# Four small reorderings in a four-layer graph kernel: tile 0's y2T, the hyperedge aggregate, layer 2's bias and the last output tile

## The chip, the cores and the metric

The kernel runs on one core of one Trainium2 chip. The metric is the device time of one execution in microseconds; the kernel before took 1214.8 us, the median of three runs from 1214.73 to 1215.12. A core has a matrix engine (TensorE, PE in the profile, with its weight loads listed as PEld), a vector engine (VectorE, DVE), a scalar engine (ScalarE, ACT), a general engine (GpSimd, POOL) and a queue that issues transfers (SyncE, SP). Each engine works through its own instructions in order and waits for the others on semaphores.

## The reference, cut to what matters

The input x has 8 batches of 2048 nodes with 64 features, and adj is a row-normalised 2048 x 2048 adjacency. Four graph layers follow each other, each with a residual and a layer norm over the 64 features:

```python
x = layernorm(x + chebyshev(x, adj))            # layer 0: out = sum_k T_k(adj) x W_k(node), k = 0, 1, 2
x = layernorm(x + hypergraph_attention(x, H, adj))   # layer 1
x = layernorm(x + x @ Ws + (adj @ x) @ Wn + bias)    # layer 2
x = layernorm(x + (A_hat @ x) @ W3.T)           # layer 3, A_hat = D^-1/2 (adj + I) D^-1/2
```

In layer 0, T_2 x = 2 adj (adj x) - x, and the weights of each node come from an embedding of 16 numbers. In layer 1, each of 64 hyperedges first gets an aggregate: the softmax-weighted mean of its nodes' features h, here a sum over nodes (`aggp`) times the reciprocal of the weights' sum (`rden`). Scores of the edges are computed from ELU(aggregate) through a linear layer and a tanh, and weight what every node takes from its edges. A second term, `industry`, is adj @ (x W_ind).

## The kernel before, in words

Nodes are cut into 16 tiles of 128 rows; a tile holds 8 x 64 = 512 columns (batch and feature). The adjacency is used as a mask of zeros and ones (`msk`, kept in DRAM for the later layers) times a row scale, and every left operand is split into a high and a low part (`y_hi`, `y_lo`), so that one product of a tile with the adjacency is 32 matmuls of 128 x 512: 16 row blocks times two parts.

Layer 0 begins with the first product y1 = adj x for all tiles (line 569), and the second product of tile 0 (line 603). Then `layer0` goes tile by tile inside `program_order()`, which fixes the order on PE, DVE, ACT and POOL as it is written. For tile 0, POOL forms mask times row scale in four quarters (`scaled_first`, line 1340) and DVE compares each with the raw adjacency (`compare_first`, line 1350), which only feeds a flag that is read at the end of the program. `second_term` (lines 1415 to 1421) transposes tile 0's y2 on PE into `try` and subtracts xT on DVE, which gives `y2T`. `weigh` (lines 1448 and 1459) then does eight groups for each tile: PE multiplies xT, y1T and y2T by the weights into a two-buffer PSUM tile `pp`, and DVE adds four slices of it to r, weighted by the embedding. The raw adjacency halves of tile 2 take the buffers of tile 0's, so they are loaded by SP once tile 0's comparisons are done. SP is not in the fixed order; the scheduler places its transfers.

Layer 0's last tile goes through `last_tile`, which ends with `rden` and the last parts of h, y_hi and y_lo (line 1599, two instructions for each half). Layer 1 starts with the list `head`, whose chain on one tile is: `agg` (line 731), exp (735), ELU (738), transpose (trhe), copy, linear layer (fche, 755), tanh, scores; pieces `0.i` and `1.i` of the industry product are put between. Its main list runs the 16 tiles as a software pipeline and ends with layer 2's projection, so that x2 holds the residual plus the self term, and with 16 POOL instructions that add layer 2's bias to x2 (line 1254).

Layer 2 and layer 3 are plain loops over the tiles, placed by the scheduler. Each step of layer 2 loads a mask tile, does 32 matmuls into `acc`, computes r on DVE (line 2029), normalises it (`layernorm`, lines 139 to 156: sum, centring, square on ACT, variance, root on ACT, reciprocal, product), and projects the tile before (`projected`: transposes tr_l, the copy xT_l at line 1994, matmuls yp at line 2008). Each step of layer 3 does 32 matmuls, r (line 2042), the same layer norm into `o`, and a store of `o` that ACT issues (line 2047).

Of the kernel before, what the change touches and what calls it, by code (L numbers as in the profile page):

```python
# [9 lines left out]
F32 = mybir.dt.float32  # L10
# [3 lines left out]
ALU = mybir.AluOpType  # L14
# [44 lines left out]
def r_(ap):  # L59
    return ap.bitcast(F32R)  # L60
# [3 lines left out]
def kernel(  # L64
# [58 lines left out]
    def b_view(t2):  # L123
        return t2.rearrange("p (b c) -> p b c", b=B)

    def bcast(small):
        return small.unsqueeze(2).to_broadcast([P, B, C])
# [484 lines left out]
    def layer1(  # L612
# [86 lines left out]
        def column_view(src):  # L699
            return src[:, 2 * P:4 * P].rearrange("p (b e) -> p b e", b=B)[:, :, 0]  # L700

        head = (
            "1.mask 2.mask 3.mask 4.mask c.agg 0.i c.hexp c.he 0.ind c.trhe c.agg1 c.heT "
            "c.fche c.sums c.the c.nagg 1.i c.sep 1.i c.serow c.sert 1.i c.ese c.eexp c.ese2 "
            "c.dnp c.ext 1.i c.rec c.hgr c.dnp2 1.i c.late "
        )
        with tc.tile_pool(name="fa", bufs=2) as fa:
# [8 lines left out]
                for n, k in (("ftr", 1), ("fmm", 1))  # L716
            )
            with program_order():
                c = {}
                low = slice(64, P)  # L720
                sums = fa.tile([P, 2, B], F32, tag="sums", name="sums", bufs=1)
                late = own.tile([P, NT - NE, 2, B], F32, tag="b0_11", name="rest_sums")
# [1 line left out]
                def parts(dst, full):  # L724

                    nc.vector.tensor_copy(r_(dst), full)
                    nc.vector.tensor_tensor(r_(dst[low]), full[low], dst[low], ALU.subtract)

                def aggregate():
                    c["agg"] = agg = fa.tile([P, BC], F32, tag="hs", name="agg", bufs=3)  # L730
                    nc.vector.tensor_tensor(b_view(agg), b_view(aggp), bcast(rden), ALU.mult)

                def exp_edges():
                    c["he"] = fa.tile([P, BC], F32, tag="xT", name="he")
# [93 lines left out]
                def other_weights():  # L828
# [1 line left out]
                    weight_sums(c["dn2"], NE, NT)  # L830

                perform(head, dict(
                    agg=aggregate, hexp=exp_edges, he=elu_edges, trhe=turn_edges, heT=turned_edges,
                    fche=fc_edges, the=tanh_edges, sep=edge_scores, serow=score_rows, sert=turn_rows,
                    agg1=lambda: parts(agg1, c["agg"]), sums=sum_edges, nagg=negated, ese=capped,
                    eexp=exp_scores, ese2=split_scores, dnp=first_weights, ext=extension,
# [274 lines left out]

        first = {}

        def layer2(j):

            t = {}

            def by_half(v):
                return v[:, j, :].rearrange("p (r h c) -> p h r c", h=2, c=C)

            def turned():
                t["tr"] = tr = ps_m.tile([P, BC], F32, tag="m", name=f"tr2_{j}")
                for pr in range(NP):
                    pc = slice(pr * P, (pr + 1) * P)
                    transpose(tr[:, pc], x2[:, j, pc])

            def kept_turned():
                t["xT"] = small("sT", f"xT2_{j}", (P, BC))
                nc.scalar.copy(t["xT"], t["tr"])

            def projected(place):
                pool, tag = dict(g=(ps_g, "g"), f=(ps_fc, "fc"))[place]
                mm = pool.tile([P, 2, BC], F32, tag=tag, name=f"u_{j}")
                t["mm"] = mm = mm.rearrange("p h (r c) -> p h r c", r=NP)
                for pr in range(NP):
                    for h in range(2):
                        rs = slice(h * 64, (h + 1) * 64)
                        nc.tensor.matmul(
                            mm[:, h, pr, :], t["xT"][rs, pr * P:(pr + 1) * P], w2_sb[rs],
                            start=True, stop=True,  # L1140
                        )

            def high():
                nc.scalar.copy(r_(by_half(i_hi)), t["mm"][:, :, :, 0:C])

            def with_self():
                nc.vector.tensor_tensor(
                    by_half(x2), t["mm"][:, :, :, C:2 * C], by_half(x2), ALU.add
                )

            def rest():
                nc.vector.tensor_tensor(
                    r_(by_half(i_lo)), t["mm"][:, :, :, 0:C], by_half(i_hi), ALU.subtract
                )

            def mask():
                first["a"] = mask_parts(own, 0, (0, 1, 2, 15), "l2")

            def times():
                if not j:  # L1160
                    first["acc"] = ps_acc.tile([P, BC], F32, tag="acc", name="a2_0")
                times_mask(first["acc"], first["a"], i_hi, i_lo, j)

            return dict(
                f=turned, xT=kept_turned, mm=projected, hi=high, add=with_self, lo=rest,
                amask=mask, A=times,
            )
# [4 lines left out]
        with program_order():  # L1172
# [77 lines left out]
                ),  # L1250
                {"rests": lambda: reciprocals(late[:, :, 0, :], late[:, :, 1, :], NE, NT)},
            )
            for j in range(NT):
                nc.gpsimd.tensor_tensor(
                    b_view(x2[:, j, :]), b_view(x2[:, j, :]),
                    bias2_sb.unsqueeze(1).to_broadcast([P, B, C]), ALU.add,
                )
        return x2, first["acc"]

    def mask_parts(own, j, homes, name):  # L1260

# [8 lines left out]
    def layer0(  # L1270
# [459 lines left out]
        def last_tile():  # L1730

            last = NT - 1
            early[0](6)
            half_features(0)
            gather(last - 1)
            denp = ps_p.tile([P, 2, 2, 4 * C], F32, tag="pp", name="denp")[:, 0, 0, 0:B]
            nc.tensor.matmul(denp, mds[last - 1], es[:, last - 1, :], start=True, stop=False)
            projected(last, 0)
            half_normed(1, 0)
            half_normed(1, 1)  # L1740
            copied(last, 0, "sc")
            weights_of(last, slice(0, 4))
            copied(last, 0, "h")
            copied(last, 0, "hi")
            half_normed(1, 2)
            half_weighted(0)
            copied(last, 0, "lo")
            early[0](3)
            half_features(1)
            early[0](1)  # L1750
            projected(last, 1)
            copied(last, 1, "sc")
            weights_of(last, slice(4, 8))
            half_weighted(1)
            early[0](1)
            half_gather(0)
            nc.tensor.matmul(denp, mds[last], es[:, last, :], start=False, stop=True)
            half_gather(1)
            nc.vector.tensor_tensor(rden, rden, denp, ALU.add)
            nc.vector.tensor_scalar(rden, rden, TINY, None, op0=ALU.max)  # L1760
            nc.vector.reciprocal(rden, rden)
            for what in ("h", "hi", "lo"):
                copied(last, 1, what)

        with program_order():
# [3 lines left out]
            quarters = [scaled_first(h) for h in range(2)]  # L1769
            compare_first(0, quarters[0])  # L1770
            mask(1, 1)
            compare_first(1, quarters[1])
            for h in range(2):
                summed(0, h)
            second_term(0)
            scaled(1, 0)
            for j in range(NT):
                when(j + 2, load_adj)
# [58 lines left out]
    def short_program(top):  # L1837
# [83 lines left out]
        with tc.tile_pool(name="l0", bufs=1) as l0, tc.tile_pool(  # L1921
# [49 lines left out]
                nc.vector.tensor_scalar(flag, bad[:, 0:1], -1.0, 1.0, op0=ALU.mult, op1=ALU.add)  # L1971


        x2, a2_first = layer1(
            own, wts, fcw_sb, fcb_sb, av_sb, fcg_sb, vecs, rden, hgr, aggp, agg_st, h_sb, y_hi,
            y_lo, mask_tile, times_mask, w2_sb, bias2_sb, ps_acc, early,
        )
# [2 lines left out]
        with tc.tile_pool(name="mj2", bufs=3) as mjp, tc.tile_pool(  # L1980
# [40 lines left out]
            for j in range(NT):  # L2021
                acc = a2_first
                if j:
# [5 lines left out]
                nc.vector.scalar_tensor_tensor(  # L2029
                    r, acc, cols_of["s1"][:, j:j + 1], x2[:, j, :], op0=ALU.mult, op1=ALU.add  # L2030
                )
                layernorm(ln, r, x2[:, j, :], f"l2_{j}")
                if j:
                    projected(j - 1)
            projected(NT - 1)
            for j in range(NT):
                a = mask_tile(mjp, j, "l3")
                acc = ps_acc.tile([P, BC], F32, tag="acc", name=f"a3_{j}")
                for mt in range(NT):
                    times_mask(acc, a, v_hi, v_lo, mt)  # L2040
# [615 lines left out]
```

## Time and profile before

| what | value |
|---|---|
| runs | 1214.73, 1214.8, 1215.12 us; median 1214.8 |
| the profiled execution | 1214.06 us, of which the span that the trace covers is 1212.4 us |
| mean granted PE clock | 0.994 of full speed |
| busy share: PE, PEld, DVE, ACT, POOL | 98%, 78%, 73%, 32%, 41% |
| HBM traffic over the span | 128 GB/s |
| landing of an adjacency half's DMA, median and longest | 3.8 and 12.5 us |
| landing of an output store, median | 2.0 us |

The page gives the share of the span in which an engine was busy. A matmul's end is modelled, so a busy PE can still be one that waits inside; the starts of its instructions tell its pace better. A line of a timeline shows when an instruction or a run of equal ones started, how long it took, its engine, its source line, what it wrote and read, and in brackets how long its engine stood idle before it and what ended that. The busy share of an engine is an average over stages with different limits; what an edit is worth is read at its own place.

### The profile page before, as it was taken

The page shows a single profiled execution, that of the slowest core. Times are in us where ns is not written, and L with a number is a line of the kernel's source. Part 1 is how long each engine was busy: PE and PEld are TensorE (multiplying, and loading weights), DVE is VectorE, ACT ScalarE, POOL GpSimd, SP SyncE. Part 2 cuts the span into 40 slices and gives each one's busy share as a digit, 9 for nine tenths or more (in the row PEclk, how much of TensorE's full clock was granted, in tenths as well). Part 3 has the DMA queues.
Part 4 walks back from the last instruction along what each step waited for, and adds up shares of the span by engine and source line. Part 5 has one row for each costly group of instructions (what it writes and reads, how often), then busy time and mean ns, then how long its engine had stood idle before and what let it go on. Part 6 is the DMA issues. An engine that isn't in the chain of part 4 may idle for free. (4 is left out here: it accounts for less than half of the span.)

```text
span 1212.4 us, 19761 instructions
## 1 busy us (share of the span) xinstructions
PE 1185.2 (98%) x7470; PEld 945.0 (78%) x7470; DVE 889.8 (73%) x1671; ACT 386.7 (32%) x1003; POOL 500.5 (41%) x429
## 2 busy tenths in 40 slices
PE   9999899999999999999999999999999999999996
PEld 7877688888888888888887766666657788888885
DVE  5555668888888888888877688988877665655554
ACT  3100101222222222222233467767777311111111
POOL 2000382555545555555521389888870700000000
PEclk9999999999999999999999899999999999999999
DMA  8987942323332233333293223223220433334451
GB/s 298 239 228 228 169 151 93 113 98 116 115 109 95 96 103 115 116 116 114 79 324 127 89 71 113 91 83 105 96 70 1 152 127 108 136 105 174 174 178 68
DMA packets 101848, 157.10 MB, mean 130 GB/s; under 512 B 13041, under 2 KB 64369, under 8 KB 96113
## 3 DMA queue, kind: packets, MB, share of 16 engines
q1 hardware_dynamic: 96944, 151.38, 38.8%
q10 hardware_dynamic: 4368, 4.33, 1.0%
q8 instruction: 61, 1.00, 0.3%
q0 software_dynamic: 432, 0.05, 0.1%
q14 instruction: 43, 0.34, 0.1%
HBM read 117.97 MB, written 37.76 MB: 128 GB/s over the span
## 5 line engine op out<-in xcount | busy, mean ns | idle before, releaser
L1459 DVE SCALAR_TENSOR_TENSOR r<-pp,emb_sb,r 128x256 f32<-128x256 f32 x512 | 247.5, 483 | 77.8 <-PE pp L1448 63.7
L1448 PE MATMUL pp<-w_sb,y2T 64*128 64x256 f32 x1024 | 153.4, 376 | 3.5 <-DVE y2T L1421 3.5
L1448 PE MATMUL pp<-w_sb,xT 64*128 64x256 f32 x1024 | 155.4, 380 | 0.6 <-DVE r L1459 0.6
L1448 PE MATMUL pp<-w_sb,y1T 64*128 64x256 f32 x1024 | 153.4, 376 | 0.0
L1317 POOL TENSOR_TENSOR ms<-msk,srow 128x1024 f32<-128x1024 f32 x30 | 76.6, 2553 | 93.7 <-DVE msk L449 93.7
L1448 PEld LDWEIGHTS pp<-w_sb,y2T 64*128 64x128 f32 x1024 | 99.2, 187 | 15.0 <-DVE y2T L1421 3.9
L1448 PEld LDWEIGHTS pp<-w_sb,y1T 64*128 64x128 f32 x1024 | 99.4, 187 | 11.2
L1448 PEld LDWEIGHTS pp<-w_sb,xT 64*128 64x128 f32 x1024 | 95.2, 187 | 12.9 <-issue 2.8
L569 PE MATMUL y1p<-x_hi,m 128*128 128x512 f32 x256 | 102.9, 402 | 0.0
L569 PE MATMUL y1p<-x_lo,m 128*128 128x512 f32 x256 | 100.6, 393 | 0.3 <-DVE x_lo L472 0.2
L1909 PE MATMUL a<-v_hi,mj_l 128*128 128x512 f32 x256 | 100.1, 392 | 0.0
L1909 PE MATMUL a<-v_lo,mj_l 128*128 128x512 f32 x256 | 100.0, 391 | 0.0
L1909 PE MATMUL a<-y_lo,mj_l 128*128 128x512 f32 x240 | 95.1, 396 | 0.0
L1909 PE MATMUL a<-y_hi,mj_l 128*128 128x512 f32 x240 | 94.9, 395 | 0.0
L1405 PE MATMUL y2p<-y_hi,msk 128*128 128x512 f32 x240 | 94.7, 395 | 0.0
L1405 PE MATMUL y2p<-y_lo,msk 128*128 128x512 f32 x240 | 93.5, 390 | 0.0
L1909 PE MATMUL ind<-y_hi,mj_l 128*128 128x512 f32 x208 | 90.5, 435 | 0.0
L1909 PE MATMUL ind<-y_lo,mj_l 128*128 128x512 f32 x208 | 81.9, 394 | 0.0
L1357 DVE SCALAR_TENSOR_TENSOR ms<-ms,adj 128x1024 f32<-128x1024 f32 x30 | 67.3, 2243 | 0.0
L968 POOL TENSOR_TENSOR ez<-ez,coef 128x1024 f32<-128x1024 f32 x32 | 61.6, 1927 | 11.1 <-DVE ez L963 11.0
L1640 POOL TENSOR_TENSOR hs<-h,es 128x512 f32<-128x512 f32 x15 | 15.7, 1043 | 116.1 <-ACT hgr L1612 116.1
L1909 PEld LDWEIGHTS ind<-y_hi,mj_l 128*128 128x128 f32 x208 | 39.3, 189 | 26.7 <-issue 17.3
(334 smaller groups left out, 2429.4 us busy)
## 6 DMA issues: line engine op xcount, KB each, us to landing
mj_l<-mask SPq DMA_DIRECT2D x44, 1024.0 KB, 4.9
adj<-in_at SPq DMA_DIRECT2D x64, 256.0 KB, 3.8
mask<-msk SPq DMA_DIRECT2D x32, 512.0 KB, 4.5
raw<-in_at SPq DMA_DIRECT2D x31, 512.0 KB, 5.6
oh<-oh SPq DMA_DIRECT2D x32, 128.0 KB, 4.1
xT<-in_xt SPq DMA_DIRECT2D x16, 256.0 KB, 3.1
xs<-in_xn SPq DMA_DIRECT2D x16, 256.0 KB, 2.7
kept<-x SPq DMA_DIRECT2D x16, 256.0 KB, 3.5
```

The source lines that it names most:

```text
L569: nc.tensor.matmul(accs[q][jj], r_(m[:, t, jj * P:(jj + 1) * P]), r_(part[:, mt, :]), start=i + h + t == 0 and part is x_hi, stop=i == 3 a ...
L968: nc.gpsimd.tensor_tensor(by_b(ezs[i]), by_b(ezs[i]), per_b(t["coef"], 2 * i, 2), ALU.mult)
L1317: nc.gpsimd.tensor_tensor(ms, m, srow[j].unsqueeze(1).to_broadcast([P, 8, P]), ALU.mult)
L1357: nc.vector.scalar_tensor_tensor(ms, ms, 1.0, raws[j][h], op0=ALU.mult, op1=ALU.not_equal, accum_out=bad[:, 2 * j + h:2 * j + h + 1],)
L1405: nc.tensor.matmul(acc, r_(msk[j, mt // 8][:, mt % 8, :]), r_(part[:, mt, :]), start=mt == 0 and part is y_hi, stop=mt == NT - 1 and part ...
L1448: nc.tensor.matmul(pp[:, h, pl, :], terms[j][name][rs, 2 * bq + pl], w_sb[rs, k, dq * 4 * C:(dq + 1) * 4 * C], start=k == 0, stop=k == K - 1,)
L1459: nc.vector.scalar_tensor_tensor(rb, ppv[:, :, dd, :], emb_sb[:, j, d:d + 1], rb, op0=ALU.mult, op1=ALU.add)
L1640: nc.gpsimd.tensor_tensor(b_view(hs), b_view(h_sb[:, j, :]), bcast(es[:, j, :]), ALU.mult)
L1909: nc.tensor.matmul(acc, r_(a[:, mt, :]), r_(part[:, mt, :]), start=mt == 0 and part is hi, stop=mt == NT - 1 and part is lo,)
```

## The change

It has four parts.

1. In layer 0, `second_term(0)` is called before the second pair of comparisons (`compare_first(1, ...)`) and after the second mask, in place of after both comparisons and the two sums on POOL.
2. The aggregate is computed in `last_tile`, directly after the reciprocal of `rden` and before the last parts of h, y_hi and y_lo. It lies in the buffer `b0_1` of the pool `own`, and `head` no longer has `c.agg`.
3. The bias of layer 2 is added on POOL to x2 for tiles 0 and 15 only, behind layer 1; for tiles 1 to 14 it is added on POOL to r, inside the loop of layer 2, between r and the layer norm.
4. The last tile of layer 3 is done in two halves of 256 columns (four batches each). Each half has its own 32 matmuls, its own layer norm on half-width tiles, and its own store; SP issues the first half's, ACT the second half's.

```diff
         head = (
-            "1.mask 2.mask 3.mask 4.mask c.agg 0.i c.hexp c.he 0.ind c.trhe c.agg1 c.heT "
+            "1.mask 2.mask 3.mask 4.mask 0.i c.hexp c.he 0.ind c.trhe c.agg1 c.heT "
...
-                c = {}
+                c = {"agg": early[2]}
...
+        def add_bias2(t):
+            nc.gpsimd.tensor_tensor(
+                b_view(t), b_view(t), bias2_sb.unsqueeze(1).to_broadcast([P, B, C]), ALU.add
+            )
...
-            for j in range(NT):
-                nc.gpsimd.tensor_tensor(
-                    b_view(x2[:, j, :]), b_view(x2[:, j, :]),
-                    bias2_sb.unsqueeze(1).to_broadcast([P, B, C]), ALU.add,
-                )
+            for j in (0, NT - 1):
+                add_bias2(x2[:, j, :])
...
             nc.vector.reciprocal(rden, rden)
+            agg = own.tile([P, BC], F32, tag="b0_1", name="agg")
+            nc.vector.tensor_tensor(b_view(agg), b_view(aggp), bcast(rden), ALU.mult)
+            early.append(agg)
             for what in ("h", "hi", "lo"):
                 copied(last, 1, what)
...
             mask(1, 1)
+            second_term(0)
             compare_first(1, quarters[1])
             for h in range(2):
                 summed(0, h)
-            second_term(0)
...
                     r, acc, cols_of["s1"][:, j:j + 1], x2[:, j, :], op0=ALU.mult, op1=ALU.add
                 )
+                if 0 < j < NT - 1:
+                    add_bias2(r)
                 layernorm(ln, r, x2[:, j, :], f"l2_{j}")
...
+            def last_half(k, a):
+                j, hb = NT - 1, B // 2
+                cols = slice(k * BC // 2, (k + 1) * BC // 2)
+                pool, tag = ((ps_acc, "acc"), (ps_mm, "mm"))[k]
+                acc = pool.tile([P, BC], F32, tag=tag, name=f"a3_{j}_{k}")[:, 0:BC // 2]
+                for mt in range(NT):
+                    for part in (v_hi, v_lo):
+                        nc.tensor.matmul(
+                            acc, r_(a[:, mt, :]), r_(part[:, mt, cols]),
+                            start=mt == 0 and part is v_hi, stop=mt == NT - 1 and part is v_lo,
+                        )
...
+                nc.vector.scalar_tensor_tensor(
+                    flat(r), acc, cols_of["sdinv"][:, j:j + 1], x2[:, j, cols],
+                    op0=ALU.mult, op1=ALU.add,
+                )
+                nc.vector.tensor_reduce(s, r, AX.X, ALU.add)
+                nc.vector.scalar_tensor_tensor(
+                    r, spread(s), -1.0 / C, r, op0=ALU.mult, op1=ALU.add
+                )
+                nc.scalar.activation(flat(sq), flat(r), AF.Square, scale=C ** -0.5)
+                nc.vector.tensor_reduce(var, sq, AX.X, ALU.add)
+                nc.scalar.activation(std, var, AF.Sqrt, bias=eps_t)
+                nc.vector.reciprocal(rstd, std)
+                nc.vector.tensor_tensor(o, r, spread(rstd), ALU.mult)
+                (nc.sync, nc.scalar)[k].dma_start(out[j * P:(j + 1) * P, cols], flat(o))
+
             for j in range(NT):
                 a = mask_tile(mjp, j, "l3")
+                if j == NT - 1:
+                    for k in range(2):
+                        last_half(k, a)
+                    break
```

In the order of instructions that results, PE, ACT and POOL keep theirs outside the last tile and the bias additions. On DVE, y2T of tile 0 stands ahead of two comparisons, `agg` ahead of the last two y_lo, and in the last tile the first half's r stands ahead of the reciprocal and the product of tile 14. On SP, the two transfers of tile 2's second adjacency half move from ahead of a row load (`srow`) and two small weight loads to behind them.

## The prediction

> **What bounds the kernel now.** I read the page's first two parts first: the share of each engine, then the slices.
>
> ```profile
> PE 1185.2 (98%) x7470; PEld 945.0 (78%) x7470; DVE 889.8 (73%) x1671; ACT 386.7 (32%) x1003; POOL 500.5 (41%) x429
> PE   9999899999999999999999999999999999999996
> PEclk9999999999999999999999899999999999999999
> ```
>
> PE is the bound nearly everywhere, so an edit pays only where PE waits, where its clock falls, or behind its last matmul. The slices show three such places: slice 4 (121 to 152 us), the 8 in the clock row (667 to 697 us) and the 6 at the end. Next came PE's waits, longest first:
>
> ```profile
> PE try L168 <- ACT deg L1436: 4.2, 15, 0.8
> PE pp L1448 <- DVE y2T L1421: 3.5, 1, 3.5
> PE trhe L168 <- issue: 1.6, 1, 1.6
> ...
> PE tr_l L168 <- DVE x L156: 0.4, 1, 0.4
> ```
>
> Columns: total, times, longest. Lines two to four are one wait each, and each is at a place that the change edits. The timelines of those places (start, length, engine, line, operation, idle before it):
>
> ```profile
> 147.73 1.74 DVE L1350 SCALAR_TENSOR_TENSOR msq<-msq,adj 128x512 f32<-128x512 f32 x1
> ...
> 149.41 1.20 DVE L1350 SCALAR_TENSOR_TENSOR msq<-msq,adj 128x512 f32<-128x512 f32 x1
> ...
> 150.54 0.68 DVE L1421 TENSOR_TENSOR y2T<-try,xT 128x512 f32<-128x512 f32 x1
> ...
> 151.28 0.70 PE L1448 MATMUL pp<-w_sb,y2T 64*128 64x256 f32 x4 [3.48 <-DVE y2T L1421]
> ```
>
> The y2T of tile 0 stands on DVE behind two comparisons that nobody waits for, although its input `try` left PE at 146.7.
>
> ```profile
> 662.11 0.49 DVE L1599 TENSOR_TENSOR y_lo<-hp,y_hi 128x128 fp32r<-128x128 f32 x2
> 662.51 0.68 DVE L731 TENSOR_TENSOR agg<-aggp,rden 128x512 f32<-128x512 f32 x1
> ...
> 952.70 1.50 DVE L140 SCALAR_TENSOR_TENSOR r<-s_l,r 128x512 f32<-128x512 f32 x1
> ...
> 956.79 1.60 DVE L156 TENSOR_TENSOR x<-r,rstd_l 128x512 f32<-128x512 f32 x1
> ```
>
> The first pair heads a serial chain (exp, ELU, transpose, fc, tanh, scores) on which PE waits. The second pair is the first layer norm of layer 2; the same two rows take 0.69 in later tiles. The stretch 943.6 to 965.0 is filled on POOL by the 16 bias additions (21.4 us).
>
> ```profile
> 1202.38 0.75 DVE L2042 SCALAR_TENSOR_TENSOR r<-a,sdinv,x 128x512 f32<-128x512 f32 x1 [2.37 <-PE a L1909]
> ...
> 1206.62 0.69 DVE L156 TENSOR_TENSOR o<-r,rstd_l 128x512 f32<-128x512 f32 x1
> 1207.35 0.34 ACTq L2047 DMA_DIRECT2D out<-o  x1
> ```
>
> After the last matmul, 4.93 us of DVE and ACT run with PE idle, then 5.1 us for the store and the program's end.
>
> [...]1.60 against 0.69 for `x<-r,rstd_l` beside POOL, while y2T, with one input in PSUM, took 0.68 with POOL busy. [...]The trace shows 112 ns start to start at 128 columns (L594) and 227 at 512[...]. [...]The trace has one stretch at 0.50, from 674.9 to 685.3[...]; the 3.48 us wait at 147.7 left the clock at 1.00, so one such gap does not decide it.
>
> **Part 1: tile 0's y2T ahead of the last two comparisons.** y2T now follows the mask at 147.73 and ends at 148.42 (0.69, no contention by the above), so PE's y2 matmuls start at 148.5 in place of 151.28: 2.8 earlier. But the two comparisons (1.74 + 1.20) now run until 151.4, ahead of the first eviction r<-pp, whose group is ready at 150.5 (y2's start plus 2.0, as before). It ends at 151.4 + 2.04 = 153.4. pp has two buffers, so the third group, which could start at 148.5 + 4.4 = 152.9, waits for it: 0.5 back. Before, that group started at 155.70. **Net -2.3.** No work is removed. The orders on PE, ACT and POOL stay; on SP one changes: tile 2's second adjacency half (two DMAs) falls behind a row load that waits for POOL until 161.2 and two small ones, so it is issued near 162.7 in place of 153. It lands 3.8 later (the median), at 167. Its mask is then late by 1.5 against a DVE that runs 2.3 ahead, and is followed by a comparison of 1.2 to 3.4 (both seen), up to 171.2; tile 1's y2T needs `try` at 171.5. Cover just holds, so I take 0; if it fails, up to 2.3 is lost. Range -2.8 to 0. Later groups keep the gain because PE is the bound up to 650.
>
> **Part 2: aggregate ahead of y_lo.** `agg` needs rden (661.90) and aggp (POOL sees it at 662.1) and starts at 662.1 in place of 662.51. The chain behind it (exp on ACT, ELU, trhe) moves by the same **-0.4**; range -0.5 to 0. The pair y_lo ends at about 663.2 in place of 662.6; the last early industry matmul, at 663.00, waits 0.2 and is covered by PE's 1.6 idle before trhe. That `agg` lies in another buffer costs nothing: its home's earlier tenant was read long before, its next (g of tile 1) is written after 685.
>
> **Part 3: layer 2's bias in the loop.** POOL adds x of tile 0 and, once it exists, of tile 15; the 14 others are added to r inside the loop, 1.29 us each. On POOL the first of those stands behind tile 15's, whose input is there at 949.7; it is wanted at 959, so nothing waits. Gain: POOL is idle during the first layer norm, so its two slow rows fall from 1.50 + 1.60 to 0.69 each, x of tile 0 comes 1.7 earlier, and PE's transpose, at 958.55, starts when its matmuls end, at 957.95: **-0.6**. Cost: in tiles 1 to 14, s waits for POOL. DVE's order there is r, xT of the tile before, s, so xT, for which PE waits, stays ahead of the new wait. In the steady tile: r ends 968.26, POOL 968.35 to 969.65, s at 969.7 in place of 968.78, v_lo of the tile before 0.3 later (its readers are in layer 3), x done near 974.1 in place of 973.67; PE transposes it at 976.07. Slack 2.0, so cost 0. Range -0.9 to +0.3.
>
> **Part 4: the last tile in halves.** PE issues 64 matmuls of 256 columns for 32 of 512. The trace has none of this kind and shape. Bounds: [...]134 ns, start to start of the fp32 rows at 128 columns (yp, 1.07 us for 8), the slowest that reload weights. I take 118: 64 x 0.118 = 7.55 against 32 x 0.227 = 7.27, +0.3. The half's chain from half-width rows: 0.48 (L1459), 0.41 (L1515), 0.43 (L1516), 0.42 (L1520), 0.42 (L1522), 0.30, 0.20, 0.42 (L1493) = 3.08, and the old chain's gaps of 0.29: 3.37 for 4.93. The second half's r is ready at 1202.6, but DVE is free only at about 1202.95: the first half's r starts at 1198.8, is interleaved with tile 14's rstd and o (0.9 us) and ACT's store of tile 14, and ends there. End of o: 1202.95 + 3.37 = 1206.3 for 1207.31, **-1.0**. The first half's store, on SP with nothing behind it, is out by 1205. The last store is half as large; its 2.0 landing is taken as unchanged. Range -1.5 to -0.2 (134 ns: r at 1203.7).
>
> **Sum:** -2.3 - 0.4 - 0.6 - 1.0 = -4.3, against the profiled execution's own 1214.06 (span 1212.4 and 1.7 around it): 1209.8. The median shown is 1214.8, 0.74 above that execution, so the forecast for a median is **1210.5**. About 0.2% (2.4 us, 1212.4) is what can be told from no change.
>
> **The rivals.** (a) Part 1's gain is eaten by the late adjacency half or by the first eviction. For it: the cover is 0.3 us thin and adjacency loads have taken up to 12.5. Against: DMA share is 0.16 from 160 to 170. Time 1210.5 + 2.0 = 1212.5. Chance 0.15. (b) The clock. The chain before the half-clock stretch gets 0.4 shorter. If PE no longer falls to half rate, up to half of 10.4 us, 5.2, is won; PE also follows the DVE and POOL chain there, so I take 3.5: 1207.0, chance 0.10. [...]1212.2, chance 0.05. (c) The change does not do what it says in the loop: s or x arrives late because POOL's addition is slow. It needs 2.0 us beyond the 1.29, and POOL's slowest was 1.74; each further 0.1 costs 14 x 0.1. At 2.2 us late a tile, 0.2 is exposed: 1213.3, chance 0.03. (d) **Slower:** the 256-column matmuls cost as much as the 512s because the weight load is not hidden. At 227 ns PE ends 7.3 later, the short chain saves 1.6 and part 4 turns to +5.7: 1214.8 - 3.3 + 5.7 = 1217.2. It makes the kernel slower from (7.27 + 1.6 + 3.3)/64 = 190 ns, by 0.2% from 227. For it: equal recorded durations at both widths (0.38 and 0.39). Against: 112 ns at 128 columns. Chance 0.04.
>
> **How the numbers follow.** Main case 0.63 (1208.8 to 1212.0 by its unknown terms), (a) 0.15, (b) 0.15, (c) 0.03, (d) 0.04. Faster by over 0.2%: 0.63, 0.15 of (b), and the lower third of (a), 0.05: 0.83, less 0.03 for the four small terms all falling short: 0.80. Slower: (d) 0.04 and 0.01 for longer half clock: 0.05. Same: 0.15. The range takes in the main case, (b) and (a), and leaves out (d) and the tails: 1206.5 to 1213.2.
>
> **What would show it.** Right: no PE wait for y2T in tile 0, at most 0.6 at the third pp group; PE's wait before trhe 1.2; no wait of tr_l for x; L140 and L156 at 0.69 in layer 2's first tile; the last o 3.4 after its r; a 256-column step of 110 to 120 ns. Wrong: a PE wait for y2T of tile 1, waits of tr_l in tiles 2 to 15, another length of the half-clock stretch, or a step above 135 ns.

## The result and the profile after

The changed kernel takes **1204.45 us** (median of 7 runs, 1202.65 to 1208.23). In the same set of runs the kernel before takes 1214.8 (7 runs, 1209.25 to 1217.68). The ratio is 0.9925, 95% interval [0.9903, 0.9947]. The forecast was 1210.5 with a range of 1206.5 to 1213.2: the sign was right, the gain was about twice the forecast, and the range was missed at its lower end. In later sets the ratio of the same two kernels was 0.9932 [0.9914, 0.9949] and 0.9954 [0.9937, 0.9972]. In both kernels the executions differ in how long PE runs at half clock (the mean granted clock is 0.992 to 0.999 in after's seven runs, 0.988 to 0.998 in before's of the later sets), and that is half of this story.

The profiled execution takes 1202.65 us, its span 1200.9. First three rows of the page after (PE busy, PE by slice, PE's clock by slice):

```profile
PE 1179.7 (98%) x7502; PEld 942.4 (78%) x7502; DVE 887.0 (74%) x1677; ACT 389.3 (32%) x1005; POOL 499.7 (42%) x429
PE   9999999999999999999999999999999999999997
PEclk9999999999999999999999999999999999999999
```

The 8 in slice 4 and the 8 in the clock row are gone. PE's waits after, longest first (total, times, longest):

```profile
PE try L168 <- ACT deg L1434: 4.2, 15, 0.8
...
PE trhe L168 <- PE ind L1670: 0.9, 1, 0.9
...
PE pp L1446 <- DVE r L1457: 0.6, 1, 0.6
```

The waits for y2T (3.5) and for x at tr_l (0.4) are gone; the one before trhe fell from 1.6 to 0.9. The timeline after, at the places that were edited (start, length, engine, line, operation, idle before it):

```profile
146.99 0.68 DVE L1419 TENSOR_TENSOR y2T<-try,xT 128x512 f32<-128x512 f32 x1
147.59 1.16 DVE L1348 SCALAR_TENSOR_TENSOR msq<-msq,adj 128x512 f32<-128x512 f32 x1
...
147.73 0.70 PE L1446 MATMUL pp<-w_sb,y2T 64*128 64x256 f32 x4
...
148.68 1.20 DVE L1348 SCALAR_TENSOR_TENSOR msq<-msq,adj 128x512 f32<-128x512 f32 x1
...
149.81 2.03 DVE L1457 SCALAR_TENSOR_TENSOR r<-pp,emb_sb,r 128x256 f32<-128x256 f32 x4
...
944.40 0.69 DVE L140 SCALAR_TENSOR_TENSOR r<-s_l,r 128x512 f32<-128x512 f32 x1
...
947.69 0.69 DVE L156 TENSOR_TENSOR x<-r,rstd_l 128x512 f32<-128x512 f32 x1
...
1192.92 0.48 DVE L2064 SCALAR_TENSOR_TENSOR r<-a,sdinv,x 128x256 f32<-128x256 f32 x1
...
1195.85 0.42 DVE L2076 TENSOR_TENSOR o<-r,rstd 128x256 f32<-128x256 f32 x1
1196.31 0.34 ACTq L2077 DMA_DIRECT2D out<-o  x1
```

y2T no longer stands behind the comparisons and PE takes it without a wait. The two rows of the first layer norm fell to 0.69. The last o ends 3.35 us after its r started.

To see where the 11.4 us of span went, I cut both timelines at the same instructions. The stages run from start to start of the named instructions, except for "end of o". Names on PE: `aggp` and `trhe` are the aggregate's sum and transpose, `fc` is layer 1's linear layer on a tile, `tr_l` and `yp` are layer 2's transpose and projection.

| stage | before | after | difference | forecast |
|---|---|---|---|---|
| start to `try` of tile 0 | 146.07 | 146.11 | 0.0 | 0 |
| `try` to third pp group (part 1) | 9.63 | 6.04 | -3.6 | -2.3 |
| third group to last aggp | 505.61 | 505.62 | 0.0 | 0 |
| aggp to trhe (part 2) | 3.71 | 3.25 | -0.46 | -0.4 |
| trhe to tile 0's first fc (clock) | 34.56 | 30.50 | **-4.06** | 0; rival (b) -3.5 |
| fc to layer 2's first tr_l (part 3) | 258.97 | 258.14 | -0.8 | -0.6 |
| first tr_l to last yp (part 3's loop) | 131.52 | 130.62 | **-0.9** | 0 |
| last yp to end of the last o (part 4) | 117.24 | 115.99 | -1.25 | -1.0 |
| end of o to the end (store) | 5.04 | 4.67 | -0.4 | 0 |

Three rows carry the surprise: the clock, layer 2's loop, and part 1. The clock first. In both kernels PE issues sixteen tiny matmuls (`dnp`, 16 columns each: the sums of the edges' weights for the 16 tiles) between groups of four 512-column industry matmuls. In before:

```profile
671.76 0.58 PE L805 MATMUL dnp<-ese,pT 64*128 64x16 f32 x4
...
673.40 1.50 PE L805 MATMUL dnp<-ese,pT 64*128 64x16 f32 x12
```

Windows view of before, cut where its clock changes, then of after at the same work (columns: busy time of PE, PEld, DVE, ACT and POOL, granted clock, DMA share, GB/s):

```profile
671.72:675.14 3.42, 3.40 (x22) 2.90 (x22) 1.10 (x6) 0.39 (x2) 0.00 (x0) 1.00 0.35 131
675.14:685.38 10.24, 10.24 (x31) 7.81 (x30) 5.68 (x18) 2.17 (x11) 4.81 (x3) 0.50 0.00 0
```

```profile
666.99:670.40 3.41, 3.38 (x21) 2.46 (x20) 1.50 (x9) 0.40 (x2) 0.00 (x0) 1.00 0.79 284
670.40:680.64 10.24, 9.87 (x52) 7.46 (x51) 7.32 (x20) 5.41 (x20) 4.76 (x3) 1.00 0.08 26
```

PE is recorded busy 3.40 of 3.42 us in the window ahead of the drop, so no wait that the profile shows precedes it. Of these 3.42 us, 57% are the sixteen dnp matmuls. From start to start one takes 0.112 us for 16 columns, where 512 columns take 0.227; at the pace of the 512, 16 columns would need 0.007 (an estimate from these figures). The clock record fits a fixed grid: in before, from PE's first full clock to the drop it is 669.01 us, which is 196 times 3.4133, and the stretch, 10.24, is three times that. In after, full clock lasts 1191.25 us, 349 times 3.4133, up to the idle end of the program. A step of this grid is called a window here. In the other profiles that are shown below the stretches are 3.42, 6.82 and 10.2 us long: one, two and three steps. The grid lies differently over the work in each: the first dnp starts 0.04 us behind a step in before, 0.75 behind one in after. So where the windows lie over dnp differs from execution to execution, and with it, by theory C below, what dnp costs.

### The profile page after: what moved, and what is told of

Same layout as the page of the kernel before. It is cut to its first block, busy times and chain, and to the rows that moved or that the text cites. A ratio compares the mean times of both kernels' runs of the same rounds, so it can differ in the third digit from the quotient of the medians.

```text
span 1200.9 us, 19838 instructions
## 1 busy us (share of the span) xinstructions
PE 1179.7 (98%) x7502; PEld 942.4 (78%) x7502; DVE 887.0 (74%) x1677; ACT 389.3 (32%) x1005; POOL 499.7 (42%) x429
## 4 chain that ended last, share of the span: by engine, by line
PE 93%; DVE 2%; ACT 2%; DMA 1%; issue 1%; POOL 0%; SPq 0%; ACTq 0%; POOLq 0%; DVEq 0%
PE pp L1446 27%; PE a L1910 19%; PE ind L1910 10%; PE y2p L1403 9%; PE y1p L569 9%; PE fc L1028 3%; PE try L168 1%; PE yp L2009 1%; PE gp L929 1%; PE trm L168 1%; PE red L978 1%; PE u L1139 1%; PE hp L1571 1%; PE dp L947 1%; ACT y L1409 1%; PE aggp L1651 1%
## 5 line engine op out<-in xcount | busy, mean ns | idle before, releaser
L1446 PEld LDWEIGHTS pp<-w_sb,y2T 64*128 64x128 f32 x1024 | 99.3, 187 | 11.4 <-DVE y2T L1419 0.3
L1910 PE MATMUL a<-v_hi,mj_l 128*128 128x512 f32 x240 | 93.9, 392 | 0.0
L1910 PE MATMUL a<-v_lo,mj_l 128*128 128x512 f32 x240 | 93.7, 391 | 0.0
L1111 POOL TENSOR_TENSOR r<-r,bias_sb 128x512 f32<-128x512 f32 x14 | 17.9, 1276 | 105.3 <-DVE r L2030 105.3
```

What stands on the lines that cost most here:

```text
L1111: nc.gpsimd.tensor_tensor(b_view(t), b_view(t), bias2_sb.unsqueeze(1).to_broadcast([P, B, C]), ALU.add)
L1446: nc.tensor.matmul(pp[:, h, pl, :], terms[j][name][rs, 2 * bq + pl], w_sb[rs, k, dq * 4 * C:(dq + 1) * 4 * C], start=k == 0, stop=k == K - 1,)
L1910: nc.tensor.matmul(acc, r_(a[:, mt, :]), r_(part[:, mt, :]), start=mt == 0 and part is hi, stop=mt == NT - 1 and part is lo,)
```

## Experiments

Theory C: an almost empty window costs the time that PE then runs at half clock, and both kernels draw lots for it at three places, tile 0's y2T wait, the chain before trhe, and dnp. The parts change the odds. Theory E: the edits alone carry the gain, and the clock is incidental.

"On" below is the share of a window in which PE runs matmuls of more than 16 columns and does not wait. Counted over the 20 kept profiles, leaving out the first 20 us: 26 windows at full clock were on for 0.42 or less, and half clock followed each of them; of 30 at 0.45 to 0.58 it followed three; of some 6800 above that it followed none. (The count takes in the windows at the program's end.) Two of the 26 are dnp windows, in before and in after_empty below: only there does it matter that tiny matmuls are not counted. A run's clock is the mean granted one; each window at half clock takes about 0.0014 off it (an estimate: half of 3.41 in some 1205 us). All runs are timed against the kernel before on the same chip, so differences hold within a set.

### First set: the dnp matmuls spread out, together, and part 1 alone

```diff
-"c.dnp c.ext 1.i c.rec c.hgr c.dnp2 1.i c.late "
+"c.dnp c.ext 1.i c.rec c.hgr c.dnp2 1.i c.dnp3 1.i c.late "    # _spread: dnp2 six, dnp3 six
+"c.dnp c.ext c.dnp2 1.i c.rec c.hgr 1.i c.late "               # _together
```

In the _spread kernels one later `1.i` is dropped for the one added. base_spread is before with it:

> The kernel before with one reordering on PE and nothing else: the twelve 16-column dnp matmuls (dnp2) are issued as six and six, with one group of four 512-column industry matmuls of tile 1 taken from later and put between and after them. Theory C (clock): the 10.4 us at half clock come from a 3.4 us window in which the 16 tiny dnp matmuls (0.58 + 1.50 us) leave the array mostly idle; spread out, no window is that empty, so the mean clock is 0.998 in all runs and the time is 5.2 below that of before where before has the stretch: 1214.8 - 5.2 = about 1209.5, all runs within 1.5 us of each other. Theory E (the edits alone carry the gain, the clock follows from PE's 1.6 us wait before trhe, which is unchanged here): the stretch stays where it is and the time is 1214.8, clock 0.994.

Measured: median 1211.08, mean 1212.0 (22 runs, 1208.24 to 1220.02); before 1212.93, mean 1213.2 (43 runs). Ratio 0.9987 [0.9971, 1.0003]. The profile shows no drop at dnp, but only half of the runs have a clock of 0.9955 or more. That fits theory C on the place, though one profile without a drop does not prove it; that it was the only place was wrong.

after_spread, after with it:

> The changed kernel with the same reordering of dnp2 and tile 1's industry matmuls. Theory C: the stretch, which the changed kernel has in some executions (clock 0.992 to 0.994, 1207 to 1208) and not in others (0.997 to 0.999, 1202.7 to 1204.5), is gone from all: clock 0.998, about 1203.5 with little spread; against base_spread the four parts are worth 1209.5 - 1203.5 = 6. Theory E: both kinds of execution stay, median 1204.5; against base_spread the four parts are worth 10.

Measured: 1203.35 (6 runs, 1202.42 to 1204.72), all at 0.997 or more. As theory C has it. Six runs are few; over all sets, 5 of 79 runs with part 1 and spread dnp are under 0.9955 (p1_spread to p14_spread, after_spread and its repeat), against 11 of 31 with dnp as it stood (after and after_filled).

> The changed kernel with the opposite reordering: the four and the twelve dnp matmuls are issued one behind the other, the industry group that stood between them behind. Theory C: 2.1 us of tiny matmuls in one piece fall into one 3.4 us window at more of its possible positions, so the half-clock stretch comes in more executions than in the changed kernel (3 of 7 seen there): most runs at 0.993 and 1207 to 1208.5. Theory E (the wait before trhe decides): the share of runs with a stretch does not change, median about 1204.5.

Measured: 1205.28 (6 runs), three at 0.994 and 1206.5 to 1207.1, three at 0.997 or more. 3 of 6 against 3 of 7: no answer. My expectation was badly made, since a window over 2.1 us of dnp in one piece holds as much on-time as one over dnp, four industry matmuls and dnp2.

p1_spread is base_spread with part 1:

> base_spread with part 1 alone (tile 0's y2T ahead of the last two comparisons). My forecast's step: -2.3, with 0.5 of the 2.8 given back at the third group. The reading of the changed kernel's trace: the two comparisons took 1.16 and 1.20 there in place of 1.74 and 1.20, the first eviction was in time and nothing was given back: -2.8 to -3.5. Rival: part of it is that the adjacency transfer before it happened to land 0.7 earlier in that execution, and the edit alone is worth 2.8 at most.

Measured: 1207.35 (22 runs), 3.7 below base_spread in the mean and 2.8 below at clocks of 0.9955 or more; 4 of 22 runs are under 0.9955, where base_spread has 11 of 22. In the trace, the third group starts 6.42 after `try`; without part 1 it is 8.96 to 9.63. Its profile caught a second place of the clock:

```profile
659.86:663.27 3.41, 1.13 (x7) 0.72 (x8) 2.44 (x5) 1.88 (x3) 0.00 (x0) 1.00 0.79 201
663.27:666.69 3.42, 3.42 (x12) 1.19 (x9) 2.11 (x4) 1.11 (x1) 0.00 (x0) 0.50 0.99 262
```

Here PE is busy 1.13 of 3.41 us: the waits before trhe (1.6) and fche (0.7) fell into one window. In before's profile the same two waits lay in two windows, on 0.56 and 0.77, and the clock stayed at 1.00. The stretch was one window, itself full (3.42 of 3.42 us busy), and cost 1.2 (trhe to sx 13.26 in place of 12.06).

### Second set: the wait filled, and parts 2, 3 and 4 on top of part 1

> base_spread with 14 matmuls of the constant ones into a spare PSUM tile, put on PE in the wait for tile 0's y2T (about 14 x 0.21 = 3 us of its 3.5): the wait itself stays, only PE no longer idles in it. Theory C (clock): the wait costs time twice, once as itself and once because a 3.4 us window that falls over it is half empty and the next runs at half clock, in about 7 of 10 positions of the windows; with the filling the second part goes: mean of the runs 1 to 2 below base_spread's 1212.0, none at a clock under 0.995 but for the chain at layer 1's head (one window, 1.7 us, in about 4 of 10). Theory E: filling a wait changes nothing, mean 1212.0 and the same spread of clocks.

Measured: 1210.6, mean 1210.5 (22 runs), none under 0.9935; before 1209.96, mean 1210.3 (54 runs). The clock rose as theory C has it (18 of 22 runs at 0.9955 or more), the time did not fall: the mean is 0.2 above before's, while base_spread on two other chips lay 1.2 and 1.8 below before's. So the forecast gain is missed, and the run does not tell the theories apart: in this profile the comparisons took 1.21 and 0.93, y2T was there at 148.5, and the filling held PE until 150.07. The wait that I filled is shorter in some executions than in the one from which I sized it.

> p1_spread with part 2 added (aggregate ahead of y_lo). My forecast's step: -0.4. Theory C: also the wait before trhe (1.63 us, with 0.68 behind it) falls by half, so that no window there is emptier than 0.45 of its length; in p1_spread's profile one window was 0.67 idle and the next ran at half clock. So the mean falls by 0.4 and 0.4 x 1.7 to 3.4 more, to about 1207.0, and no run but an outlier is at a clock under 0.996. Theory E: -0.4 alone, 1207.9, with the same spread as p1_spread.

Measured: 1205.89 (15 runs), 14 of them at 0.996 or more. aggp to trhe is 3.25 for 3.70. No p1_spread ran on this chip, so the size rests on the trace: -0.45.

> p1_spread with part 3 added (layer 2's bias inside its loop). My forecast's step: -0.6, all of it ahead of the first transpose of layer 2. The trace of the changed kernel reads -0.6 there and 0.067 less in each of the next tiles (8.765 in place of 8.83 from transpose to transpose, 0.9 in all): tr_l to tr_l at 8.76 here says that the loop's shortening belongs to this part, and the time is then -1.5. If the pitch stays 8.83, it comes from another part and this one is worth -0.6.

Measured: 1205.54 (18 runs). Transposes are 8.767 apart in place of 8.83; first tr_l to the fifteenth is 122.76 for 123.5, and the stage ahead of the first 258.05 for 258.65. Part 3 owns the loop's gain.

> p1_spread with part 4 added (last tile in two halves). My forecast's step: -1.0 up to the end of o, nothing on the store. The trace of the changed kernel reads -1.25 from the first matmul of the last tile to the end of o, and 0.5 less from there to the end: -1.75 here, spans read in the trace the same way. Rival: the 0.5 of the store is chance, and the last 4.6 to 5.1 us vary as much from run to run.

Measured: 1204.99 (12 runs). Last yp to the end of o 116.00 for 117.2; end of o to the end 4.68. Over all profiles the latter is 4.48 to 4.77 in the ten with halves and 4.90 to 5.23 in the ten without: the 0.4 is not chance. The last store's size is what differs there. In this profile both comparisons ran at full length (1.78 and 1.20) and the third group started at 6.40 in place of 5.93: the give-back of 0.5 exists.

### Third set: dnp emptied, the kernel itself, and one wait less

```diff
-"c.dnp c.ext 1.i c.rec c.hgr c.dnp2 1.i c.late "  ...  "... 0.sx 0.gp0
+"c.dnp c.ext c.dnp2 c.rec c.hgr c.late "          ...  "... 0.sx 1.i 1.i 0.gp0
```

> The changed kernel with both groups of four industry matmuls taken out from between and behind the sixteen tiny dnp matmuls and issued behind tile 0's sx: dnp, dnp2 and sx then stand in one stretch of about 3 us without a 512-column matmul. Theory C: with the fraction of a 3.4 us window that PE spends on 512- or 128-column work under about 0.45, the next window runs at half clock; here that holds for about 8 of 10 positions, so most runs lie at 1206 to 1209 with a clock of 0.992 to 0.995, and the profile shows the drop at the end of a window that lies over dnp. Theory E: the same work in another order, no PE wait added of more than 0.5 us: 1204.5, clock as in the changed kernel.

Measured: 1204.56 (6 runs), three at 0.995, three at 0.997; after_again 1203.17. The profile shows the drop where theory C puts it:

```profile
670.65:674.06 3.41, 2.98 (x23) 2.44 (x21) 1.81 (x11) 0.71 (x3) 0.00 (x0) 1.00 0.76 267
674.06:677.48 3.42, 3.42 (x12) 2.94 (x12) 1.69 (x8) 0.84 (x4) 0.78 (x1) 0.50 0.00 1
```

The window ahead of the drop is on for 0.22. Place right, price and frequency too high: a stretch of one window costs 1 to 2 us, not 4 (the runs at 0.995 lie 1.8 above those at 0.997 in the mean; p1_spread's stretch cost 1.2).

> The changed kernel itself, for a direct comparison on the chip of this set. Theory C: two kinds of runs as before, about one in three with a stretch at dnp (clock 0.992 to 0.995, 3 to 4 us longer), the others at 0.997 or more. Against the kernel before, runs with no stretch on either side: -6.

Measured: 1203.17 (6 runs, 1201.55 to 1203.87), all at 0.997 or more. In the fourth set (after_third) 5 of 10 runs are below 0.9955.

> The changed kernel with dnp2 split and an industry group between the halves, as in after_spread. Theory C: no run with a stretch, clock 0.997 to 0.999 in all; mean 1 below after_again's mean, and equal to its runs without a stretch or up to 0.6 above (the reordering costs 0.55 between trhe and the first fc in the traces). Theory E: same mean as after_again.

Measured: 1203.01 (6 runs). No gain over after_again, and its profile has a one-window drop at 663.08, behind a window that is on for 0.54, over the wait before trhe. So spreading dnp is no better version: it pays 0.55 always for what it saves sometimes.

```diff
+if j == 4:
+    seen = l2p.tile([P, 1], F32, tag="seen", name="seen")
+    nc.vector.tensor_tensor(seen, r[:, 0:1], x2[:, NT - 1, 0:1], ALU.add)
```

> p1_spread with one DVE operation of one column added in layer 2, behind tile 4's centring, that reads tile 15's x after POOL's last bias addition. The bias stays ahead of the loop. From tile 5 on DVE's r then has no wait for POOL left, only that for PE; in tiles 0 to 4 it has both. Theory W (the second wait costs 0.067 us in each tile, and part 3 took it away): transposes 8.83 apart in the tiles up to 4 and 8.765 in those from 6 on. Rival (the shorter pitch comes from POOL's work in the loop, or from s being late): 8.83 in all tiles.

Transposes of tiles 2 to 5 in the timeline of wait_once:

```profile
979.64 0.60 PE L168 MATMUL tr_l<-ident,x 128*128 128x128 f32 x4
...
988.48 0.60 PE L168 MATMUL tr_l<-ident,x 128*128 128x128 f32 x4
...
997.29 0.60 PE L168 MATMUL tr_l<-ident,x 128*128 128x128 f32 x4
...
1006.05 0.60 PE L168 MATMUL tr_l<-ident,x 128*128 128x128 f32 x4
```

They are 8.84 and 8.81 apart, then 8.76, and 8.76 on average up to tile 14: theory W, to the tile. With the bias ahead of the loop each r waits for PE and for POOL (whose addition is long done), in after for PE alone. The second wait costs 0.067 us for each tile here: r starts 0.107 us behind the tile's last matmul in before and 0.038 in after, and passes that on to xT_l (0.667 behind r in both) and so to yp on PE (0.736 behind xT_l in both). The time of this run, 1218.4, had another cause, which the next set takes up: L140 of tile 0 took 11.32.

### Fourth set: part 3 undone, and what POOL does to DVE

> The changed kernel with part 3 alone undone: the sixteen bias additions stand ahead of layer 2's loop again. From the stage tables: 0.6 to 0.8 more ahead of layer 2's first transpose and 0.067 more in each of the next tiles, 0.9 in all, so +1.5 against after_third. Theory L (POOL's row of additions can hold off DVE's first centring until it is through, as in wait_once, where it took 11.3 us in place of 1.5): a few of the runs, about one in ten, lie 9 to 12 above the others with a clock near 0.993. Rival: the 11.3 us came from the operation added in wait_once, and no run lies apart here.

Measured: 1205.58 (17 runs); two lie apart, 1216.12 and 1218.44. Without these the mean is 1205.55, for 1204.89 in after_third (standard error 0.6): +0.7, not distinct from the 1.5, nor from nothing. One of the two is the profiled one:

```profile
944.09 0.69 DVE L139 TENSOR_REDUCE s_l<-r 128x8 f32<-128x512 f32 x1
944.81 11.38 DVE L140 SCALAR_TENSOR_TENSOR r<-s_l,r 128x512 f32<-128x512 f32 x1
...
935.76 19.87 POOL L1250 TENSOR_TENSOR x<-x,bias_sb 128x512 f32<-128x512 f32 x16
```

The same instruction that takes 0.69 alone and 1.50 in before's profile ends 0.6 after POOL's sixteen additions are through (955.6). In wait_once it likewise ends 0.6 after them (956.46 and 955.91). PE waits 9.4 us for x, and its clock is at half for three windows, 955.2 to 965.4. Theory L holds for both long runs of which there is a profile.

> The kernel of wait_once once more. Theory L: the long centring is chance, so most runs lie near p1_spread's less 0.7 (the pitch in tiles 5 to 14, 10 x 0.067), and the profile shows L140 at 1.5. Rival: it comes from the added operation, which holds DVE in layer 2's first tile, and all runs lie 10 higher.

Measured: 1207.86 (20 runs, 1206.76 to 1209.69), L140 at 1.47 in its profile: chance, not the added operation. Its transposes repeat theory W: 8.82 to 8.84 apart from tile 1 to tile 4, then 8.74 to 8.76. Over all kernels with the additions ahead of the loop, 8 of 168 runs lie some 10 above their neighbours; of 73 with the bias in the loop (after, after_filled and the like) none does. That points to part 3, but numbers so small can still be chance (a run in 20 against none in 73), and six of the eight have no profile. Before itself may have such runs too (its longest took 1223.46); its spread does not let them be counted.

> The changed kernel with one group of four industry matmuls of tile 1 taken from behind the first sx pair and put into PE's 0.68 us wait for heT at layer 1's head. It takes 0.93, so fche starts 0.26 later, and PE has 0.68 less idle there. If nothing behind it needed that group as cover: 0.3 to 0.6 below after_third, and fewer windows under half full at the head. If the chain's delay of 0.26 is passed on, or PE waits where the group stood: no difference.

Measured: 1203.9, mean 1203.7 (8 runs, 1201.51 to 1205.73); after_third 1204.61, mean 1204.9. trhe to fc is 29.99 for 30.50 in after: the forecast 0.5. The runs do not separate the two (the means' standard errors are 0.6 each).

> The changed kernel itself, as the comparison on the chip of this set: about 1203 where no window is empty at dnp, up to 4 more where one is.

Measured: 1204.61 (10 runs), five at 0.997 or more (mean 1203.2), five at 0.992 to 0.994 (mean 1206.6).

### Fifth set: the y2T wait made longer

```diff
+for _ in range(4):
+    nc.vector.tensor_copy(quarters[1][0], quarters[1][1])
 for h in range(2):
     summed(0, h)
 second_term(0)
```

> base_spread with four more DVE copies of a dead 128x512 tile (0.4 to 1.8 us each) between the comparisons and tile 0's y2T, so that PE's wait for it grows from about 3.5 to about 6 us. Theory C: at every position a 3.4 us window now lies mostly over that wait, so the profile shows PE's clock at 0.50 for one or more windows from 150 to 158 us on, in each run, and the time grows by more than the wait: the 2 to 3 us longer wait and 1.2 or more for the clock. Theory E: the clock stays at 1.00 at this place, as it did in the profiles of before and base_spread, and the time grows by the wait alone.

```profile
147.98:151.40 3.42, 0.00 (x0) 0.00 (x0) 3.35 (x6) 0.00 (x0) 3.26 (x4) 1.00 0.64 193
151.40:158.22 6.82, 4.17 (x20) 3.39 (x22) 2.87 (x5) 0.00 (x0) 6.43 (x8) 0.50 0.92 264
158.22:161.64 3.42, 3.42 (x36) 3.01 (x34) 2.47 (x6) 0.00 (x0) 3.42 (x3) 1.00 0.00 0
```

Measured: 1214.63 (17 runs), 16 of them under 0.9955, against base_look's 1208.72. The wait grew from 3.48 to 6.86, the third group came 5.4 later than in before (15.05 for 9.63): 2.0 more than the wait grew. That is the clock: in the two windows at 0.50 PE is busy for 4.17 us, of which full clock would save half, 2.1 (an estimate).

> base_spread again, for the comparison on this chip and for one more profile. Theory C: where the windows happen to lie over the y2T wait, the profile shows a drop at about 150 us; where two share it half and half, as in the profiles seen, none. In the runs, those with a clock under 0.9955 are about half, as in the first set (11 of 22).

Measured: 1208.72 (20 runs), 8 under 0.9955, and no drop in its profile: the y2T wait was 1.3 us there. So no profile shows the 3.5 us wait itself with a drop behind it. That it draws lots too is inferred from late_spread and from the runs' clocks, and was not seen.

## Why the prediction was too high, step by step

The profiled executions lie 11.4 us apart, 7.1 more than my 4.3. Of these 7.1, the clock is 4.06, part 1 is 1.3 (0.7 of it luck), layer 2's loop 0.9, the last store 0.4, and the sizes of parts 2, 3 and 4 another 0.5.

The 10.3 between the medians of the first set is in part the draw: in two later sets, on other chips, the same kernels lie 8.4 (1211.58 and 1203.17) and 6.4 apart (1210.97 and 1204.61). My starting point of 1214.8 was itself a draw, of three runs with long half clock or of that chip; the medians of before in five other sets are 1209.96 to 1212.93.

**Part 1, -2.3 forecast, -3.6 in the stage table.** The 2.8 was right: where the second mask, on which y2T stands, comes equally late after `try`, the third group starts 2.9 earlier with part 1. With the mask as late as in before's profile that is 9.63 without part 1 and 6.70 with it (after_spread_again, mask 0.1 earlier); with the mask 0.7 and 0.8 earlier it is 8.96 (base_spread) and 6.04 (after). Failed: the give-back. I took the comparison at the 1.74 that it took in before's profile; it ran at 1.16 in after's profile and at 0.67 to 1.78 in others, and the 0.5 was lost only where it ran long (p14_spread). The other 0.7 is luck: the adjacency transfer, for which the mask waits, landed earlier in after's execution (tile 0's first mask starts at 140.44 there and at 141.14 in before, in both behind a wait for it). The wait removed is no constant: in base_look, where that mask starts at 139.25, it is 1.3 in place of 3.5, and the stage without part 1 is 7.40. Rival (a)'s late half did not happen: PE had no wait for y2T of tile 1.

**Part 2, -0.4: right** (-0.45 wherever it is in). It may have an unpriced effect on the clock, as the wait before trhe is shorter (0.9 for 1.6): four of ten profiles without part 2 have a window there that is on for 0.30 to 0.33, and none of ten with it is below 0.53. But a drop follows there in three of the ten with part 2 (all on for 0.54; after_third is one) and in four of the ten without. The runs lean to it: on one chip 13 of 15 with part 2 (p12_spread) are at 0.9965 or more, against 16 of 30 (p13_spread, p14_spread). That part 2 makes drops rarer is thus likely, not shown.

**The clock, put into rival (b) with a chance of 0.10 for -3.5: this step failed.** Its size in the profiles was 4.06, near the rival's. (b)'s second case, longer half clock at 1212.2, put 1.7 on it, which was my estimate; the one-window stretch in p1_spread's profile cost 1.2. What was wrong is the main case, which took before's half-clock stretch over unchanged. I read one stretch at one place (10.24 us by its record, not 10.4) and tied it to the chain's idle. It followed a window full of tiny matmuls that count as busy, and the chain before trhe draws lots as well, as by inference does the y2T wait. Over the five chips on which before ran beside my kernels, 77 of its 188 runs have a clock below 0.9935; of 23 runs of after, 3. In runs at 0.9965 and above the two kernels are at 1207.4 and 1203.2 (means), 4.1 apart, close to the 4.3 of my sum. That is a coincidence: the trace gives the edits 6.6 (2.9, 0.45, 0.7, 0.9, 1.25 and 0.4), and before's runs at such a clock are presumably those with a short y2T wait, like base_look's. The rest of the gain is largely half-clock time. That part 1 makes it rarer, the runs show (p1_spread against base_spread); for part 2 it is likely, and for the long runs that part 3 would remove, the counts point that way.

**Part 3, -0.6: right ahead of the loop (-0.6 to -0.8), wrong inside it.** "Slack 2.0, so cost 0" held for the cost, and no tr_l waited. The step missed a gain: the loop lost one of two waits on each r, 14 x 0.067 = 0.9. And "1.50 + 1.60" is one draw of what DVE takes beside POOL's additions: nine of the eleven profiles with the additions ahead of the loop have 1.47 to 1.50 for the first of the two rows, the other two 11.3 and 11.4.

**Part 4, -1.0: right in mechanism,** -1.25. The 256-column step is (1192.60 - 1185.08)/63 = 0.119 for my 0.118, which was an estimate (64 matmuls have 63 steps); rival (d) is dead. My slow bound of 134 ns was a misreading: the yp matmuls start 0.112 apart, with 0.213 once in each row of eight. DVE came free 0.24 earlier than I took it. "Its 2.0 landing is taken as unchanged" failed: the time behind o is 0.4 shorter with the half-size last store (5.04 and 4.63, means of ten profiles each).

Rival (c), a late s, did not appear: the wait for POOL (0.86 per tile) ends 2 us ahead of PE's need.

## What to carry to other kernels

In these runs a wait of PE cost itself and, where a window was on for 0.42 or less, the half clock that followed (26 of 26 windows, those at the program's end among them). A run of tiny matmuls in which PE looked busy brought that half clock too: before's dnp window was busy for 3.40 of 3.42 us and on for 0.42. Before an edit is priced from one profile, ask what in that profile was drawn by lot (a DMA's landing, the clock's windows, DVE beside POOL), and give the edit's effect on the odds a term of its own. Beside sixteen POOL additions in a row (19.9 to 21.4 us), a DVE step on the critical path took 1.47 to 1.50 or 11.3 to 11.4 us; with fourteen of them in the loop it took 0.69. Where a kernel has such a row, breaking it up is worth a try.

## What the runs showed of the hardware that I had not expected

- DVE's scalar_tensor_tensor of 128x512 (L140 in layer 2's first tile) took 0.69 us with POOL idle (after), and beside a row of POOL additions 1.47 to 1.50 (nine profiles) or 11.3 to 11.4 (wait_once and after_no3). In these two it ended 0.6 behind POOL's row.
- In before, PE's clock fell behind a window in which PE was recorded busy 3.40 of 3.42 us, 57% of it with 16-column matmuls. The stretch was one window in p1_spread and after_empty, where PE was busy 3.42 of 3.42 us in the next, and three in before, where a third of each of the next two was tiny matmuls.
- A second engine to wait for, long since done, cost layer 2's loop 0.067 us for each tile (8.83 and 8.765 from transpose to transpose in before and after; wait_once and wait_twice repeat it).
- In the 20 profiles half clock followed every full-clock window that was on for 0.42 or less (26 of 26), three of 30 at 0.45 to 0.58, and none above. In before, a 3.48 us wait that two windows shared (on 0.50 and 0.48) left the clock at 1.00.
